# A graph-attention kernel: the residual's bias moves from the DMA queue to the vector engine, the residual tiles move to other buffers, and the instruction planner is revised

## The chip, the cores and the metric

The kernel runs on one core of a Trainium2 chip. The metric is device time in microseconds, from the start of the program to its end; lower is better. The engines are named as in the profile: PE is the tensor engine, DVE the vector engine, ACT the scalar engine, POOL the general-purpose engine, SP the engine that does nothing but issue transfers. [...]

## The reference, cut to what matters

There are 32 graphs of 512 nodes with 512 features. Each graph is normalized, goes through two attention layers, and is added to its input. All arithmetic is in float32.

```python
def gat_layer(x, mask, W, a_src, a_dst, bias, concat):
    xl = (x @ W).reshape(B, N, H, F)
    asrc = einsum('bnhf,hf->bnh', xl, a_src); adst = einsum('bnhf,hf->bnh', xl, a_dst)
    e = leaky_relu(asrc[:, :, None, :] + adst[:, None, :, :], 0.2)
    attn = softmax(where(mask[..., None], e, -1e9), axis=1)
    return einsum('bsdh,bshf->bdhf', attn, xl) (+ bias, heads side by side or averaged)

h = maximum(layernorm(x), 0)
h = elu(gat_layer(h, mask, W1, ..., b1, concat=True))     # 4 heads of 256 features
h = gat_layer(h, mask, W2, ..., b2, concat=False)         # 1 head of 512 features
out = x + h                                               # so out = (attn2 @ xl2) + x + b2
```

## The kernel before, in words

**The work of a graph.** Everything is held in tiles of 128 rows (partitions). A graph goes through four products: `project1` (features by W1, for four heads), `gather1` (attention weights `p` by projected features, per pair of heads), `project2` and `gather2` (the same for the second layer). Nearly all of them are done with seven block products in place of eight, so DVE prepares sums of blocks ahead of a product and PE's partial results are combined as they leave the accumulator banks. In `gather1` the function `sums1` writes two sums of the weights of each head into the buffers `t` (four of them, two heads at a time). In the second layer `sums2` writes sums of `p` into `hs` and differences of the projected features into the buffers `x`.

**The softmax weights.** `Soft.first` computes row scores (buffers `l`, tile `low`) on ACT and DVE, `Soft.second` forms `p`. Row vectors are spread over the partitions through DRAM: a small write and a broadcast read (`das<-as` and `as<-das`, `drr<-rr` and `rr<-drr`), on SP. In most places the mask is added to `p` by a transfer that accumulates, from a copy in DRAM (`p<-dm`, issued on POOL); then ACT takes the exponential.

**The residual.** `residual(b)` loads the four 128-row tiles of the input graph into buffers `xr` on SP, then adds `b2` to each by an accumulating transfer on POOL that reads the 2 KB row of `b2` for all 128 partitions. `gather2` adds each partial product from its accumulator bank into the tile, in place (`xr<-mm,xr` in the profile), and SP writes the tile out. The `xr` buffers (four) also serve `elu` as scratch. For graph 30 other buffers are used, and there DVE adds `b2` already. `residual` runs for all graphs; 124 tiles of 128 go through the path with the accumulating transfer.

**The banks.** In `sevens`, product 3 of a block accumulates in the bank of product 5, so its matmuls may start only when DVE has added product 5's result into the residual tile.

**The rounds.** The loop over `i` works on three graphs at a time: `gather1` of graph i+1, `project1` of i+2, `gather2` of i, `project2` of i+1. A round has 28 + 28 block products of two matmuls each, 14 of four and 14 of two, which makes 196 matmuls. Each matmul shows as two records in the trace.

**The order.** Nothing is issued as it is written down. Every step goes into `Program` as a job with an engine, an assumed duration, and what it reads and writes. `Program.order` then plans: PE's jobs stay in program order; the jobs of the other engines are ranked by how late they may start (`backwards`), placed by a forward pass in time (`forwards`), and this is repeated 12 times; the order with the earliest planned end is issued. The assumed durations and latencies are constants in the code:

```python
CROSS, SAME = 0.15, 0.1
DMA_LEAD, DMA_TAIL, DMA_RATE = 1.2, 1.0, 280e3
```

Of the kernel before, what the change touches and what calls it, by code (L numbers as in the profile page):

```python
# [19 lines left out]
P = 128  # L20
# [24 lines left out]
class Program:  # L45
# [5 lines left out]

    CROSS, SAME = 0.15, 0.1
    DMA_LEAD, DMA_TAIL, DMA_RATE = 1.2, 1.0, 280e3

# [21 lines left out]
    def latency(self, a, b):  # L76

        if self.jobs[a][0] != self.jobs[b][0]:
            return self.CROSS
        return 0.0 if self.jobs[a][0] == "PE" else self.SAME  # L80

    def forwards(self, rank):

        jobs, after = self.jobs, self.after
        n = len(jobs)
        left = [len(job[2]) for job in jobs]
        ready_at, start, landed = [0.0] * n, [0.0] * n, 0.0
        free, soon, ready = defaultdict(float), defaultdict(list), defaultdict(list)
        tensor = deque(j for j in range(n) if jobs[j][0] == "PE")
        for j in range(n):  # L90
            if not left[j] and jobs[j][0] != "PE":
                heappush(soon[jobs[j][0]], (0.0, j))
        done = []
        while len(done) < n:
            j, t = self.next_job(rank, free, soon, ready, tensor, left, ready_at)
            start[j] = t
            free[jobs[j][0]] = t + jobs[j][1]
            done.append(j)
            if jobs[j][4] is not None:
                landed = max(landed, t + jobs[j][1] + self.DMA_LEAD) + jobs[j][4] / self.DMA_RATE  # L100
            for s in after[j]:
                if jobs[j][4] is not None:
                    r = landed + self.DMA_TAIL
                else:
                    r = t + jobs[j][1] + self.latency(j, s)
                ready_at[s] = max(ready_at[s], r)
                left[s] -= 1
                if not left[s] and jobs[s][0] != "PE":
                    heappush(soon[jobs[s][0]], (ready_at[s], s))
        return start, done  # L110

    def backwards(self, rank):
# [9 lines left out]
        while True:  # L122
            for j in found:
                if jobs[j][4] is not None:
                    moving = max(moving, ready_at[j]) + jobs[j][4] / self.DMA_RATE
                    ready_at[j] = moving + self.DMA_LEAD
                if jobs[j][0] != "PE":
                    heappush(soon[jobs[j][0]], (ready_at[j], j))
# [13 lines left out]

    def next_job(self, rank, free, soon, ready, tensor, left, ready_at):

        best = None
        for e in ("PE", "ACT", "DVE", "POOL", "SP"):
# [6 lines left out]
            elif soon[e]:  # L153
                t = max(free[e], soon[e][0][0])
            else:
                continue
            if best is None or t < best[0]:
                best = (t, e)
# [10 lines left out]
    def order(self):  # L169
# [8 lines left out]
        for j in reversed(range(n)):  # L178
            later = self.DMA_LEAD + self.DMA_TAIL + (jobs[j][4] or 0.0) / self.DMA_RATE
            need[j] = max(  # L180
# [6 lines left out]
            if jobs[j][0] == "PE":  # L187
                if pe is not None:
                    need[j] = max(need[j], need[pe] + jobs[pe][1])
                pe = j  # L190
        rank, best, self.tried = need, None, []
        for _ in range(self.ROUNDS):
            back = self.backwards(rank)
            late = [-back[j] - jobs[j][1] for j in range(n)]
            start, done = self.forwards(late)
            end = max(start[j] + jobs[j][1] for j in range(n))
            self.tried.append(end)
            if best is None or end < best[0]:
                best = end, start, done, late
            rank = [-start[j] - jobs[j][1] for j in range(n)]  # L200
        _, self.start, done, self.late = best
        return done

    def emit(self):
# [5 lines left out]
def tile_gat(  # L210
# [113 lines left out]
    def accumulate(size, reads, writes, to, at, cost=0.95):  # L324
        prog.add(
            "POOL", cost, reads, writes,
            lambda: nc.gpsimd.dma_start(to, at, accum_op=OP.add), 1.4 * size,  # L327
        )
# [25 lines left out]
    def weights1():  # L354
        for c in range(2):
            for r in range(2):
                for k in range(KQ):
                    row = (r * KQ + k) * P
                    ix = AT[r, c]
                    dma(  # L360
                        256e3, (), [("w1", ix, k)], w1_sb[:, ix, k, :, 2:],
                        w1[row : row + P, :].rearrange("p (j c f) -> p c j f", j=H // 2, c=2)[:, c],
                    )

    def scores1():

        vk, bc = ps_.take()
        for a, v in enumerate((as1, ad1)):
            for j in range(H // 2):
                dma(  # L370
                    256e3, (), [vk + ("v", a, j)], bc[:, 2 * a + j, :],
                    bass.AP(tensor=v.tensor, offset=v.offset + j * 2 * FH, ap=[[0, P], [1, 2 * FH]]),
# [21 lines left out]
    def weights2():  # L394

        for (r, c), ix in AT.items():
            dma(
                512e3, [("ht", 0, 0)], [("w2", ix)], w2_sb[:, ix, :, 1 - c : W2H - c],
                w2[r * HF // 2 : (r + 1) * HF // 2, c * DO // 2 : (c + 1) * DO // 2].rearrange(
                    "(k p) f -> p k f", p=P  # L400
                ),
            )
        dma(4e3, (), ["b1"], b1_sb[:, 0], b1.rearrange("(c p) -> p c", p=P))
        dve(TINY, ["b1"], ["b1"], nc.vector.tensor_scalar_mul, b1_sb[:, 1], b1_sb[:, 0], -1.0)
        dma(256e3, (), ["b2"], b2_sb, rows_of(b2, P))
        for a, v in enumerate((as2, ad2)):
            lk, bc = ls.take()
            dma(256e3, (), [lk], bc, rows_of(v[0], P))
            for (r, c), ix in AT.items():
# [24 lines left out]
    def load(b):  # L434
        XT[b] = []
        for t in range(NT):
            xk, xt = xs.take()
            dma(256e3, (), [xk], xt, x[b, t * P : (t + 1) * P, :])
            XT[b].append((xk, xt))

    def masks(b):

        for t in range(NT):
            ak, a = adjs.take()
            dma(256e3, (), [ak], a, adj[b, t * P : (t + 1) * P, :])
            dve(
# [10 lines left out]
        if b < B - 1:  # L457
            MASK[b] = mk, md = mds.take()
            dma(512e3, every, [mk], md.rearrange("p t n -> p (t n)"), m.rearrange("p t n -> p (t n)"))
        tk, mt = mts.take()  # L460
# [4 lines left out]
            ),  # L465
            300e3,
        )
# [22 lines left out]
    def norm_turn(b, t):  # L490
# [3 lines left out]
        act(  # L494
            0.62, [xk, sk + (t,)], [xk], hn, hn, AF.Relu,
            bias=st[:, t, S : S + 1], scale=st[:, t, S + A : S + A + 1],
# [13 lines left out]
        else:  # L510
# [3 lines left out]
            act(  # L514
                1.14, [xk], [ak], words.rearrange("p (h f) -> p h f", h=2),
                hn.bitcast(U16).rearrange("p (f h) -> p h f", h=2), AF.Copy,
# [6 lines left out]
                ),  # L523
                200e3,
            )
            act(
                1.14, [xk], [("ht", t, 0), ("ht", t, 1)],
                ht[:, :, t * P : (t + 1) * P].bitcast(U16).rearrange("p k (n h) -> p h k n", h=2),
# [14 lines left out]
    class Soft:  # L543
# [7 lines left out]
        def spread(self, v, keys, rows, to, through):  # L551
# [11 lines left out]
            dma(  # L563
                0, [ok], [dk], dr[:k].rearrange("k (b j) -> b k j", j=32),
                bass.AP(
# [4 lines left out]
            dma(  # L570
                256e3 * rows, [dk], [ok], o[:, :rows].rearrange("p r n -> p (r n)"),
                bass.AP(tensor=dr.tensor, offset=dr.offset, ap=[[0, P], [1, rows * N]]),
# [67 lines left out]
        def second(self, h):  # L640
# [19 lines left out]
            if not here:  # L660
                mk, md = MASK[self.b]
                for us in (0, 1), (2, 3):
                    keys = p_keys(pk, us)
                    accumulate(
                        500e3, keys + [mk], keys,
                        *(t[:, us[0] : us[-1] + 1].rearrange("p t n -> p (t n)") for t in (p, md)),
# [67 lines left out]
    def sevens(left, right, rkeys, put, kh, units, width, order):  # L734
# [3 lines left out]
        for u, n in order:  # L738
            m = units[u][0]
            acc, first = {1: "a", 2: "g", 5: "b", 6: "a", 7: "a", 3: "b", 4: "a"}[n], n in (1, 2, 5)  # L740
            if first:
# [4 lines left out]
            pe(  # L746
                akeys + rkeys(n), [bk], kh * width / 597,
                [
# [48 lines left out]
    def project1_first(zt):  # L797

        for j in range(H // 2):
            zk, z = zt[j]  # L800
            for t in range(NT):
                for c in range(2):
# [5 lines left out]
                           for q in (("w1", AT[r, c], k), ("w1s", AT[r, c], k, j))],  # L808
                        [bk], KT * 0.435,
                        [  # L810
# [29 lines left out]

    def elu(g, places, at, cost):

        keys = [("h1", g, r) for r in range(2)]
        ek, e = xrs.take()
        act(cost, [*places, "b1"], [ek], e, at, AF.Exp, bias=b1_sb[:, 0, g : g + 1], scale=-1.0)
        act(0.54, [ek], [ek], e, e, AF.Relu, bias=1.0, scale=-1.0)
# [6 lines left out]
    def gather1_plain(soft, heads):  # L853

        for h in heads:
            pk, p = soft.p.pop(h)
            for f in range(FPH):
                bk, ps = banks.take()
                for s in range(NT):
# [8 lines left out]
                    )  # L868
                elu(h * FPH + f, [bk], ps, 0.6)
                banks.give(bk)  # L870
# [50 lines left out]
    def gather1(soft, j):  # L921
# [4 lines left out]
        for i, n in PAIR:  # L926
# [5 lines left out]
            if first:  # L932
# [4 lines left out]
            pe(  # L937
                akeys + wkeys, [bk], KQ * M / 597,
                [
# [17 lines left out]
            if n in (3, 4):  # L957
                elu(g, [("h1", g, q) for q in range(2)], h1[:, g, :], 0.54)
        for i in range(2):
# [51 lines left out]

    def residual(b, places=(xrs,) * NT):

        XR[b] = []
        for d in range(NT):
# [5 lines left out]
            halves = [xk, xk + (0,), xk + (1,)]  # L1021
            dma(256e3, (), halves, xr, x[b, d * P : (d + 1) * P, :])
            if places[0] is xrs:
                accumulate(256e3, [xk], halves, xr, rows_of(b2, P))
            else:
                dve(0.59, [xk, "b2"], halves, nc.vector.tensor_add, xr, xr, b2_sb)
            XR[b].append((places[d], xk, xr))
# [27 lines left out]
    def gather2(b, soft, blocks, order=LAST):  # L1055
# [4 lines left out]
        def put(n, u, bk, ps):  # L1060
# [7 lines left out]
            if n == 4 or r == 0 and upper[u[0]] == 0:  # L1068
                upper[u[0]] = -1
                dma(256e3, [xk, xk + (0,), xk + (1,)], (), out[b, d * P : (d + 1) * P, :], xt)  # L1070
                place.give(xk)
# [9 lines left out]
    def gather2_plain(b, soft):  # L1081
# [3 lines left out]
        for d in range(NT):  # L1085
# [8 lines left out]
            dve(0.6, [bk, xk], [xk], nc.vector.tensor_add, xr, ps, xr)  # L1094
            dma(256e3, [xk], (), out[b, d * P : (d + 1) * P, :], xr)
            banks.give(bk)
# [166 lines left out]
```

## Time and profile before

| | |
|---|---|
| runs | 2850.74, 2859.48, 2864.90 us, median 2859.48 |
| profiled execution | 2858.04 us, of which 2856.2 us from the first to the last instruction |
| busy | PE 2774.1, DVE 2584.4, ACT 2306.4, POOL 416.7 us |
| mean granted PE clock | 0.992 |
| transfers | 527.23 MB; the queue fed by POOL moves 191.92 MB |
| DRAM read | 344.72 MB |
| residual bias transfers | 124 of 256 KB, median 5.8 us from issue to landing |
| mask transfers | 304 of 512 KB, median 5.1 us |

The page of a profile gives busy times, a strip of 40 slices, the transfer queues, the chain that ended last, and the costliest groups of instructions. The line number of a group is that of a helper (L333 issues all matmuls, L319 all DVE work, L316 all ACT work, L322 plain transfers, L327 accumulating ones), so groups are told apart by their tiles: `out<-in`, with buffer numbers left out. The tile `xl2` of the second layer shows as `xl`. "Idle before" is the time an engine stood still ahead of an instruction, with the engine and tile whose end released it. A matmul's end is modelled, and a few matmul records are missing.

### The profile page before, as it was taken

Reading aid. Unit: us, or ns where it says so; the run is one execution under the profiler, and the core shown is the slowest. Engines: PE = TensorE matmul, PEld = TensorE weight load, DVE = VectorE, ACT = ScalarE, POOL = GpSimd, SP = SyncE. Lnnn points to the kernel's source line nnn. Section 1 sums busy time; section 2 is a strip of 40 time slices with the busy share of each in tenths; the row PEclk is TensorE's granted clock in tenths of the full one; section 3 lists DMA queues with packets and bytes.
Section 4 is the critical chain, followed back from the end, with each engine's and each line's share of the span. In section 5 each row is a group of like instructions: output and inputs, shape, how many; then the busy total and the mean of one; then the engine's idle time right before and its main releaser. Section 6 shows DMA issues by size and latency. Waiting matters only on the chain. (4 is left out here: it accounts for less than half of the span.)

```text
span 2856.2 us, 41534 instructions
## 1 busy us (share of the span) xinstructions
PE 2774.1 (97%) x12456; PEld 2365.5 (83%) x12456; DVE 2584.4 (90%) x6567; ACT 2306.4 (81%) x4861; POOL 416.7 (15%) x466
## 2 busy tenths in 40 slices
PE   7999999999999999999999999999999999999997
PEld 6668888888888888888888888888888888888875
DVE  7979998989999989899898999999998999999995
ACT  6878798888888888887888888888888888888872
POOL 0011111111111111111111111111111111111100
PEclk9999999999999999999999999999999999999999
DMA  6577777687786777776777877778767778777724
GB/s 204 150 174 182 188 203 188 180 193 194 181 210 181 194 185 191 201 191 182 189 188 182 207 176 183 202 190 206 190 179 194 189 187 215 176 192 191 182 68 128
DMA packets 389455, 527.23 MB, mean 185 GB/s; under 512 B 227184, under 2 KB 231280, under 8 KB 389232
## 3 DMA queue, kind: packets, MB, share of 16 engines
q1 hardware_dynamic: 327600, 332.68, 41.7%
q0 software_dynamic: 61632, 191.92, 30.3%
q8 instruction: 99, 1.62, 0.2%
q14 instruction: 124, 1.02, 0.1%
HBM read 344.72 MB, written 50.79 MB: 138 GB/s over the span
## 5 line engine op out<-in xcount | busy, mean ns | idle before, releaser
L333 PE MATMUL mm<-w_sb,hs 128*128 128x257 f32 (+1 forms) x3024 | 693.2, 383 | 19.4 <-ACT xl L316 10.8
L333 PEld LDWEIGHTS mm<-w_sb,hs 128*128 128x128 f32 x3024 | 574.0, 191 | 113.6 <-ACT xl L316 20.0
L327 POOL DMA_DIRECT2D p<-dm x304 | 267.5, 882 | 2032.1 <-DVE p L319 1034.3
L316 ACT ACTIVATE l<-as,z 128x512 f32<-128x512 f32 x640 | 441.8, 723 | 113.6 <-DMA as<-das 101.7
L316 ACT ACTIVATE l<-l,low 128x512 f32<-128x512 f32 x640 | 459.5, 723 | 71.5 <-DVE low L319 69.0
L316 ACT ACTIVATE p<-p,z 128x512 f32<-128x512 f32 x640 | 432.8, 722 | 103.4 <-DMA p<-dm 75.2
L333 PE MATMUL mm<-p,xl 128*128 128x256 f32 (+1 forms) x2016 | 489.5, 391 | 6.4 <-ACT p L316 3.5
L319 DVE SCALAR_TENSOR_TENSOR p<-rr,z 128x512 f32<-128x512 f32 x640 | 457.8, 745 | 37.2 <-DMA rr<-drr 36.8
L333 PE MATMUL mm<-w_sb,ht 128*128 128x258 f32 x2112 | 481.5, 382 | 2.2 <-ACT xl L316 1.2
L333 PE MATMUL mm<-w_sb,h 128*128 128x257 f32 x2056 | 470.0, 380 | 6.2 <-DVE h L319 4.3
L319 DVE CUSTOM_DVE_ANT_1 l<-l,mt 128x512 f32<-128x512 f32 x640 | 427.4, 683 | 46.2 <-ACT l L316 44.8
L333 PEld LDWEIGHTS mm<-w_sb,ht 128*128 128x128 f32 x2112 | 400.5, 190 | 64.1 <-ACT xl L316 4.0
L333 PEld LDWEIGHTS mm<-p,xl 128*128 128x128 f32 x2016 | 382.9, 190 | 82.6 <-issue 19.4
L333 PEld LDWEIGHTS mm<-w_sb,h 128*128 128x128 f32 x2056 | 389.9, 190 | 65.7 <-DVE h L319 5.3
L316 ACT ACTIVATE xl<-mm 128x258 f32<-128x258 f32 (+2 forms) x752 | 281.7, 384 | 49.0 <-PE mm L333 46.5
L319 DVE TENSOR_TENSOR xl<-xl,mm 128x258 f32<-128x258 f32 x558 | 224.8, 417 | 36.6 <-PE mm L333 28.7
L316 ACT ACTIVATE h<-mm 128x256 f32<-128x256 f32 x480 | 175.4, 379 | 84.2 <-PE mm L333 82.0
L316 ACT ACTIVATE xr<-h,b_sb 128x512 f32<-128x512 f32 x240 | 171.5, 723 | 77.3 <-DVE h L319 76.8
L333 PE MATMUL mm<-t,hs 128*128 128x256 f32 x960 | 218.3, 380 | 1.2 <-ACT h L316 0.9
L333 PEld LDWEIGHTS mm<-t,hs 128*128 128x128 f32 x960 | 183.1, 191 | 27.0 <-ACT h L316 1.3
L319 DVE TENSOR_TENSOR xr<-mm,xr 128x256 f32<-128x256 f32 (+1 forms) x424 | 170.9, 417 | 28.4 <-PE mm L333 19.9
L319 DVE SCALAR_TENSOR_TENSOR h<-h,b_sb,xr 128x512 f32<-128x512 f32 x240 | 175.9, 745 | 20.0 <-ACT xr L316 19.2
(105 smaller groups left out, 3427.6 us busy)
## 6 DMA issues: line engine op xcount, KB each, us to landing
p<-dm POOLq DMA_DIRECT2D x304, 512.0 KB, 5.1
rr<-drr SPq DMA_DIRECT2D x160, 512.0 KB
x<-in_x_dram SPq DMA_DIRECT2D x129, 256.0 KB
adj<-in_adj_dram SPq DMA_DIRECT2D x128, 256.0 KB
as<-das SPq DMA_DIRECT2D x64, 512.0 KB
xr<-in_x_dram SPq DMA_DIRECT2D x124, 256.0 KB
xr<-in_L_gnn_b_dram POOLq DMA_DIRECT2D x124, 256.0 KB, 5.8
out_dram<-xr SPq DMA_DIRECT2D x124, 256.0 KB
```

Source lines behind the costliest of these rows:

```text
L316: prog.add("ACT", cost, reads, writes, lambda: nc.scalar.activation(*a, **k))
L319: prog.add("DVE", cost, reads, writes, lambda: f(*a, **k))
L327: lambda: nc.gpsimd.dma_start(to, at, accum_op=OP.add), 1.4 * size,
L333: f(*a, **k)
```

## The change

Three things are changed.

1. `residual` puts its tiles into the `t` buffers, those of the weight sums of the first layer's `gather1`, in place of `xr`. 
2. `b2` is added to them by DVE (128x512, float32) in place of the accumulating transfer. `b2` is then read from its tile in on-chip memory.
3. The planner gets other constants (durations of transfers in microseconds, latency by pair of engines, transfer lead and tail), a limit on how far ahead transfers are issued, and 40 further passes in which the jobs that caused a planned standstill of PE are ranked earlier. The best of all passes is issued.

Products, their order on PE, and the number of ACT and SP instructions are unchanged: PE 6238, ACT 4223, SP 1233 instructions in both builds; DVE goes from 6505 to 6629, POOL from 471 to 347.

```diff
-    CROSS, SAME = 0.15, 0.1
-    DMA_LEAD, DMA_TAIL, DMA_RATE = 1.2, 1.0, 280e3
+    CROSS, SAME = 0.15, 0.07
+    PAIRS = {("PE", "ACT"): 0.21, ("PE", "DVE"): 0.21, ("DVE", "POOL"): 0.58, ("POOL", "DVE"): 0.4}
+    DMA_LEAD, DMA_TAIL, AHEAD = 0.8, 2.0, 3.5
...
-            j, t = self.next_job(rank, free, soon, ready, tensor, left, ready_at)
+            j, t = self.next_job(rank, free, soon, ready, tensor, left, ready_at, landed - self.AHEAD)
...
+    def sooner(self, rank, start, cause):
+        jobs, lost, free = self.jobs, {}, 0.0
+        for j in range(len(jobs)):
+            if jobs[j][0] != "PE":
+                continue
+            gap, free = start[j] - free, start[j] + jobs[j][1]
+            d = cause[j]
+            while gap > 0.05 and d is not None and start[j] - start[d] < self.SPAN:
+                lost[d] = max(lost.get(d, 0.0), gap)
+                d = cause[d]
+        return [r - self.GAIN * lost.get(j, 0.0) for j, r in enumerate(rank)]
+
+    SPAN, GAIN = 60.0, 2.0
...
+            if e in ("SP", "POOL"):
+                t = max(t, hold)
...
+        _, start, _, cause, rank = best
+        for _ in range(self.REPAIRS):
+            rank = self.sooner(rank, start, cause)
+            start, cause = look(rank)
...
+    REPAIRS = 40
...
-    def residual(b, places=(xrs,) * NT):
+    def residual(b, places=(ts_,) * NT):
...
-            dma(256e3, (), halves, xr, x[b, d * P : (d + 1) * P, :])
-            if places[0] is xrs:
-                accumulate(256e3, [xk], halves, xr, rows_of(b2, P))
-            else:
-                dve(0.59, [xk, "b2"], halves, nc.vector.tensor_add, xr, xr, b2_sb)
+            dma(0.75, (), halves, xr, x[b, d * P : (d + 1) * P, :])
+            dve(0.59, [xk, "b2"], halves, nc.vector.tensor_add, xr, xr, b2_sb)
```

Of the jobs' assumed durations, some are changed too: a plain 256 KB transfer from 0.91 to 0.75 us, the mask transfer of 512 KB from 2.5 to 2.2 us, the transposing ones from 0.71 to 1.27 and from 1.07 to 2.5 us, and four ACT jobs.

## The prediction

> **What bounds the kernel now.** I read the busy times first, then PE by slices, then who ended PE's waits in the steady stretch, then single waits in the order of time.
>
> ```profile
> PE 2774.1 (97%) x12456; PEld 2365.5 (83%) x12456; DVE 2584.4 (90%) x6567; ACT 2306.4 (81%) x4861; POOL 416.7 (15%) x466
> ```
>
> PE is the bound and DVE is next. PE's 82 us of idle time are not spread evenly, as three of the 40 slices show (columns: PE, PEld, DVE, ACT, POOL busy with records, clock, transfers):
>
> ```profile
> 428.40:499.80 71.40, 67.53 (x303) 57.93 (x302) 63.17 (x160) 57.15 (x119) 11.83 (x13) 0.98 0.73 188
> 1642.30:1713.70 71.40, 67.96 (x303) 57.82 (x302) 64.56 (x167) 57.14 (x132) 10.88 (x12) 0.98 0.70 176
> 2356.40:2427.80 71.40, 71.40 (x331) 62.37 (x330) 66.31 (x167) 59.91 (x125) 13.51 (x15) 1.00 0.84 215
> ```
>
> A slice without a wait holds 331 records, 0.2157 us each. The first slice shows 3.9 us idle but lacks 28 records, 6.0 us: a wait costs more than it shows, since the matmuls after it are slower. The steady stretch is 214.2 to 2713.4 us, rounds 1 to 29; PE idles 36.7 us there. One matmul comes once a round, the first of `mm<-xl,hs` in `gather2`: from 373.83 to 2641.05 us it passes 26 rounds, **87.2 us each**. 392 records at 0.2157 us are 84.6 us, so a round loses 2.6 us and 29 rounds lose 75 us, twice the idle time shown. From 1948.02 to 2033.05 a round took 85.03 us, so the chip can do one with hardly a wait. PE's waits in this stretch (us in total, times, longest):
>
> ```profile
> PE mm L333 <- DVE hs L319: 13.1, 5, 3.6
> PE mm L333 <- DVE xr L319: 11.8, 17, 2.3
> PE mm L333 <- ACT xl L316: 5.7, 12, 0.9
> PE mm L333 <- ACT h L316: 5.0, 6, 1.8
> PE mm L333 <- ACT p L316: 0.2, 1, 0.2
> ```
>
> The second row is followed back in one round (timeline of POOL, DVE, PE):
>
> ```profile
> 1155.39 0.86 POOL L327 DMA_DIRECT2D xr<-in_L_gnn_b_dram  x1 [7.13 <-DMA xr<-in_x_dram]
> 1159.62 0.42 DVE L319 TENSOR_TENSOR xr<-mm,xr 128x256 f32<-128x256 f32 x1 [2.00 <-DMA xr<-in_L_gnn_b_dram]
> 1160.10 1.13 PE L333 MATMUL mm<-xl,hs 128*128 128x256 f32 x4 [2.34 <-DVE xr L319]
> ```
>
> POOL waits for x, the bias transfer lands some 4 us later, DVE's addition waits for it, and product 3 waits for DVE to clear product 5's bank. In the built order 10.3 us of DVE work (mostly 9.5 to 11.5) stand between the `elu` that frees `xr` and the first addition into it. A load (issued by 1147.22, awaited by POOL until 1155.39, so up to 8.2 us) and a bias transfer (5.8 us median) don't fit. The first row, at 458.38, 1330.22, 1683.56 and 2204.52 us (10.8 us), comes from the same place: POOL's queue then holds the layer-2 mask transfers between bias transfers, `p` lands late, ACT's exponential and DVE's sums into `hs` follow late.
>
> [...]0.98 where 3.4 to 3.9 us are idle, 1.00 elsewhere. [...]the trace has 684 to 685 ns for graph 30's bias additions, but neighbours start 0.60 us apart (2816.60, 2817.20, 2817.80), and that is the price. [...]mask and bias share POOL's queue; its 191.92 MB are 304 x 512 KB + 124 x 256 KB.
>
> **The change part by part.** PE's order is the same, instruction by instruction, so all differences are in when its operands come.
>
> *Removed:* 124 bias transfers. POOL loses 124 x 0.90 = 111 us of issuing, which covers nothing (POOL is 15% busy). Its queue loses 32.5 of 191.9 MB. The chain above ends with the load. I let `DVE xr` fall from 11.8 to 1 us, and `DVE hs` from 13.1 to 4 (bounds 1 and 10: the mask transfers still take 5.1 us).
>
> *Added:* 124 DVE additions x 0.61 = 76 us; 116 serve rounds 0 to 28, 71 us, or 2.44 a round. DVE idles 190.1 us in the steady stretch, 6.6 a round, and the additions lie in that. In the order nearly all stand 7 to 15 us of DVE work ahead of their first use, so they are not on the path of PE unless DVE is full or x is late. If x is late, the addition holds up everything behind it on DVE, sums for PE among it. From the release of `t` by PE (product 6 of `gather1`) to the addition, PE and DVE work in the order leaves 8.7 to 13 us, in one round 5.1 to 6.2; against 8.2 us for a load at worst this exposes 0 to 3 us in one round. Graph 0's four fall where DVE waits 0.8 to 2.0 us for each matmul group at 34 to 42 us; their four loads go before the adjacency loads of the head, bounded at +3 us, taken as 0.
>
> *Moved to `t`:* on SP the four loads now wait for PE, and `as<-das` and the mask copy stand behind them in most rounds. ACT's waits for `as<-das` (88.9 us in the stretch) may grow; ACT has 420 us idle there, so 0. The next `sums1` must wait until the tile is written out: 5.4 us of DVE work or more stand between. A write is not timed by the page; the last one ends the span 2.7 us after its issue, so 0, upper bound 1 us a round.
>
> *The planner:* its effect shows only in the order. For each matmul of rounds 1 to 29 that waits for DVE, I summed the DVE work from DVE's own last waits for PE up to the awaited instruction, and took off the PE work between. Before, the DVE work is larger in 44 of 1049 places, after in 7 of 1128, the additions included. For ACT it is 0 and 2. So waits set by DVE's queue are mended; waits set by transfers are not in this count. I let PE's waits on ACT fall from 10.9 to 8, and add 4 for new ones.
>
> Sum for the rounds: 36.7 - (1 + 4 + 8 + 4) = 19.7 us less idle; each counts twice (75/36.7 = 2.0), **39 us**.
>
> *The end:* before the last product PE waits 7.98 us for the weights of graph 31. SP held that chain up:
>
> ```profile
> 2805.93 0.52 SPq L322 DMA_DIRECT2D das<-as  x1
> 2809.32 3.79 SPq L322 DMA_DIRECT2D out_dram<-xr  x3
> 2813.20 0.38 SPq L322 DMA_DIRECT2D as<-das  x1
> ```
>
> In the new order `as<-das` directly follows `das<-as`: it saves 4 to 5 us. Against that, around `gather1` of graph 31 (2749 to 2763 us) the count above grows from 6.9 to 8.7 us. Net 2 us saved, bounds 5 saved and 2 lost. The head is taken as 0, bounds 4 either way.
>
> Sum: 2858.0 - 39 - 2 = 2817 against the profiled execution's own time; the median of the runs is 1.4 us above that: **2818 us**. About 0.5% is what a measurement of this kernel can tell from no change: 14 us, so 2845 and 2874 are the borders.
>
> **The rivals.**
>
> *The bound passes to DVE (slower).* Of DVE's 190 us idle in the rounds only 36.0 are waits for PE (`xl` 21.0, `xr` 4.7, `h` 3.8, `p` 3.3, `hs` 3.2); the others are latency, as 40.4 for ACT's `l` and 31.0 for `rr<-drr`. If these stay, 71 us of additions fill only the 36, and 35 come on top, with PE's waits kept in another place: 2858 + 35 = 2893. It decides as soon as DVE's idle time, less the additions, cannot sink below 6.6 - 2.4 = 4.2 us in a round of 87.2. For it: DVE would be over 95% busy. Against it: the additions have 10 us of leeway and can stand in latency waits, and the order's count fell.
>
> *The waits change their releaser (no difference).* Mask transfers, not bias transfers, set `hs`; the additions wait for x where DVE waited for the bias. Then `xr` alone falls, by about half: 6 us x 2, less nothing at the end, 2847; with 1 or 2 us more at the head, 2849. For it: the `p<-dm` row of 5.1 us stays. Against it: in all of the long waits bias transfers stood beside the masks.
>
> *The planner's passes do nothing.* Then the order would be as late as before: the 44 to 7 speaks against it, and its time is that of the case before this.
>
> **How the numbers follow.** Forecast 0.72, no difference 0.16, DVE bound 0.12. The forecast's own range is 2791 (all 29 rounds at 85.03, so 29 x 2.17 = 63, and 5 at the end) to 2840 (hs and ACT mended by half, 2 lost at the end). The range of 8 in 10 reaches on over the case of no difference: 2791 to 2858; it leaves out the DVE case and a little below. Faster by over 0.5%: 0.73, within 0.16, slower 0.11.
>
> **What would show it.** Right: no row of bias transfers on POOL, its queue at about 159 MB; `DVE xr` (now `DVE t` on `xl,hs`) near 1 us; DVE busy about 2660 us; rounds of 85.9 us; the last wait of PE near 3 to 4 us. Wrong: DVE waiting for `t<-in_x_dram` by more than 20 us in total; `DVE hs` still above 10; rounds above 87.

## The result and the profile after

The change makes the kernel faster: **2807.54 us** as the median of four runs (2807.30 to 2816.68), against 2856.45 us for four runs of the kernel before on the same chip; the ratio is **0.9834, 95% interval 0.9801 to 0.9867**. The forecast was 2818 us with a range of 2791 to 2858. The profiled execution took 2807.30 us against 2858.04 us, 50.7 us less; the sum of the prediction had said 41.

I read the page of the kernel after first: engines, the queue that POOL feeds, and the mask transfers (the last column is the median from issue to landing, in us).

```profile
PE 2758.2 (98%) x12456; PEld 2364.6 (84%) x12456; DVE 2640.6 (94%) x6691; ACT 2307.5 (82%) x4861; POOL 311.7 (11%) x342
...
q0 software_dynamic: 43776, 159.40, 24.0%
...
p<-dm POOLq DMA_DIRECT2D x304, 512.0 KB, 5.3
```

PE stays the bound. POOL's queue carries only the mask transfers, and they land no sooner than before (5.3 against 5.1 us), with a sixth of the queue's bytes taken away. DVE is busy 56 us longer.

Next PE's waits in the steady stretch of the kernel after, 214 to 2665 us (us in total, times, longest):

```profile
PE mm L368 <- DVE hs L354: 3.4, 3, 1.9
PE mm L368 <- DVE h L354: 1.3, 2, 1.0
PE mm L368 <- ACT h L351: 0.7, 2, 0.4
PE mm L368 <- DVE xl L354: 0.6, 2, 0.3
PE mm L368 <- ACT xl L351: 0.5, 2, 0.3
PE mm L368 <- DVE t L354: 0.4, 2, 0.3
PE mm L368 <- ACT p L351: 0.2, 1, 0.2
```

That is 7.1 us where 35.8 us were. All sources of before have shrunk, and DVE's `h` and `xl` are new with 1.9 us together: the bank's wait for the residual (`xr`, now `t`) from 11.8 to 0.4, `hs` from 13.1 to 3.4, those on ACT from 10.9 to 1.4 us.

**Where the 50.7 us lie.** The first matmul of `mm<-x,hs` in each round marks the rounds in PE's timeline. Before, 28 rounds pass from 197.35 to 2636.24 us, 87.1 us each; after, from 191.49 to 2587.36 us, 85.57 us each. So the rounds save 2438.89 - 2395.87 = 43.0 us, the head 197.35 - 191.49 = 5.9 us, and what follows the last mark up to the end of the span 1.9 us (219.96 less 218.04). After the change 17 of the 28 rounds take 85.0 or 85.1 us; before, 3 did.

**DVE, with four more additions in a round.** One stretch of nearly eleven rounds in the kernel after (busy times of PE, PEld, DVE, ACT, POOL with records, then clock, transfer share, GB/s):

```profile
981.90:1893.60 911.70, 911.70 (x4203) 797.17 (x4202) 882.34 (x2216) 778.07 (x1641) 111.10 (x121) 1.00 0.70 184
```

PE has no idle time and DVE is 96.8% busy: of 85 us it idles 2.7. Its own waits tell what the additions displaced. First two rows of the kernel before (214 to 2713 us), then four of the kernel after (200 to 2620 us):

```profile
DVE l L319 <- ACT l L316: 40.4, 65, 1.9
DVE p L319 <- DMA rr<-drr: 31.0, 33, 2.6
```

```profile
DVE xl L354 <- PE mm L368: 19.7, 43, 1.0
DVE l L354 <- ACT l L351: 8.8, 19, 1.5
...
DVE t L354 <- DMA t<-in_x_dram: 5.8, 7, 2.0
...
DVE p L354 <- DMA rr<-drr: 4.8, 7, 1.8
```

The waits for ACT's `l` and for the broadcast `rr` were latency: while one operand was under way DVE stood still. They lost 58 us together. The additions have taken their place, and x is late for them by 5.8 us in all. DVE's waits for PE on `xl`, which the rival of a DVE bound wanted to see filled first, are hardly touched (21.0 and 19.7).

### The profile page after: what moved, and what is told of

The parts are those of the page before. It is cut to its first block, busy times and chain, and to the rows that moved or that the text cites. A ratio compares the mean times of both kernels' runs of the same rounds, so it can differ in the third digit from the quotient of the medians.

```text
span 2805.4 us, 41284 instructions
## 1 busy us (share of the span) xinstructions
PE 2758.2 (98%) x12456; PEld 2364.6 (84%) x12456; DVE 2640.6 (94%) x6691; ACT 2307.5 (82%) x4861; POOL 311.7 (11%) x342
## 4 chain that ended last, share of the span: by engine, by line
PE 85%; DVE 7%; ACT 3%; DMA 3%; issue 1%; SPq 0%; POOL 0%; DVEq 0%; ACTq 0%; POOLq 0%
PE mm L368 85%; DVE p L354 2%; ACT l L351 1%; DMA x<-adj 1%; DVE h L354 1%; DMA rr<-drr 1%; DVE l L354 1%; DMA p<-dm 1%; DVE hs L354 1%; DVE t L354 1%; ACT p L351 1%; DVE xl L354 0%; ACT adj L351 0%; ACT xl L351 0%; ACT xr L351 0%
## 5 line engine op out<-in xcount | busy, mean ns | idle before, releaser
L368 PE MATMUL mm<-w_sb,hs 128*128 128x257 f32 (+1 forms) x3024 | 690.9, 383 | 11.8 <-ACT xl L351 7.1
L354 DVE TENSOR_TENSOR t<-mm,t 128x256 f32<-128x256 f32 (+1 forms) x424 | 171.5, 416 | 15.6 <-PE mm L368 14.9
L368 PE MATMUL mm<-xl,p 128*128 128x256 f32 (+1 forms) x752 | 181.6, 391 | 4.2 <-ACT p L351 4.0
```

Source lines behind the costliest of these rows:

```text
L354: prog.add("DVE", cost, reads, writes, lambda: f(*a, **k))
L368: f(*a, **k)
```

## The experiments

All twelve runs, each with its ratio to the kernel before on the same chip (e8_end_only ran once and has none). On the other chips the kernel before had medians of 2862.34 to 2866.68 us, so ratios are compared, not medians. The mean round is that between the marks in its profile. The last column is the count of the prediction, made from the built order: places in rounds 1 to 29 where the DVE work ahead of an awaited instruction exceeds PE's work beside it (a dash: not given). The expectations give microseconds on the scale of the first chip, so they are best read by ratio, times 2856.45 us: e3_same_order_no_bias then lies at the lower edge of its rival's range, and only e13_pool_add falls clearly outside all of its ranges.

| run | what differs | median us | ratio (95%) | round us | places |
|---|---|---|---|---|---|
| before | | 2856.45 | 1 | 87.1 | 44 |
| after | | 2807.54 | 0.9834 (0.9801, 0.9867) | 85.57 | 7 |
| e3_same_order_no_bias | before, bias transfers not issued | 2851.04 | 0.9958 (0.9943, 0.9972) | 86.98 | 44 |
| e12_no_addition | after, additions not issued | 2811.81 | 0.9809 (0.9787, 0.9832) | 85.45 | 7 |
| e1_planner_only | new planner, old residual | 2869.81 | 1.0025 (1.0010, 1.0039) | 87.66 | 91 |
| e2_residual_only | old planner, new residual | 2854.25 | 0.9963 (0.9949, 0.9977) | 86.56 | 41 |
| e4_dve_bias_in_xr | after, residual in `xr` | 2835.03 | 0.9907 (0.9880, 0.9934) | 86.99 | – |
| e5_pool_bias_in_t | after, bias by transfer | 2846.43 | 0.9941 (0.9924, 0.9958) | 86.57 | 30 |
| e6_no_repairs | after, no further passes | 2823.02 | 0.9864 (0.9826, 0.9901) | 85.75 | 29 |
| e7_repairs_only | after, old constants | 2823.62 | 0.9860 (0.9807, 0.9913) | 86.23 | 5 |
| e11_gain1 | after, other passes | 2806.74 | 0.9792 (0.9768, 0.9816) | 85.51 | 3 |
| e9_two_ops | after, a second DVE operation | 2866.24 | 1.0010 (0.9992, 1.0029) | 87.15 | – |
| e13_pool_add | after, POOL adds | 2940.66 | 1.0258 (1.0234, 1.0282) | 89.85 | 45 |
| e8_end_only | before, one step moved at the end | 2865.59 | one run | 87.41 | 44 |

### Are the bias transfers what PE waited for? (e3_same_order_no_bias)

```diff
-                accumulate(256e3, [xk], halves, xr, rows_of(b2, P))
+                prog.add("POOL", 0.95, [xk], halves, lambda: None, 1.4 * 256e3)
```

> The kernel before, every engine in its old order, but the 124 bias transfers are planned and not issued; b2 is left out of the output. No addition takes their place on DVE. It is the price of the transfers alone. Theory: PE's waits for xr additions (11.8 us) and for hs in gather2 (10.8 us) go almost wholly, some 20 us idle, counted twice: 2815 to 2825 us. Rival, the order of DVE's own work sets those waits: 2845 to 2857 us, with the once-a-round wait of mm<-xl,hs still there.

The order of all other instructions stays that of the kernel before. Measured: 2851.04 us, 0.42% less (0.28 to 0.57%), about 12 us, not 39. PE's waits in 214 to 2660 us, and three of the long ones in PE's timeline (start, duration, ..., idle before and its releaser):

```profile
PE mm L333 <- DVE hs L319: 12.0, 5, 3.0
PE mm L333 <- ACT xl L316: 10.8, 13, 2.6
PE mm L333 <- DVE xr L319: 7.6, 12, 1.3
```

```profile
460.66 3.72 PE L333 MATMUL mm<-x,hs 128*128 128x256 f32 x16 [2.53 <-DVE hs L319]
...
1686.92 3.72 PE L333 MATMUL mm<-x,hs 128*128 128x256 f32 x16 [2.96 <-DVE hs L319]
...
2204.45 5.12 PE L333 MATMUL mm<-x,hs 128*128 128x256 f32 x16 [2.72 <-DVE hs L319]
```

In the kernel before these three matmuls waited 3.63, 3.00 and 2.72 us, at 458.38, 1683.56 and 2204.52 us. So with no bias transfer anywhere the same places still wait for `hs`, the first of them 1.1 us less. The row of `xr` falls from 11.8 to 7.6 us. DVE's own waits tell what is left of it: before, DVE waited 7.8 us for bias transfers, in nine places, and here it waits for no transfer of the residual, for x neither. So the 7.6 us come from the other work and waits that stand ahead in DVE's order. The size of the fall is not sharp, since one execution differs from the next: e8_end_only, with the bias transfers and the same order in these rounds, shows 16.4 us for this row. In the profiled execution here (2856.07 us, one of the slower of its 20) the wait for ACT's `xl` is 10.8 us (5.7 before, 8.2 in e8_end_only), and PE's waits come to 35.7 us, as in the kernel before. Most of the waits belong to the order; the transfers stood beside them and added a part. The waits at the head (6.12 us at 51.96, 4.25 at 115.57, 4.10 at 186.97) are those of the kernel before too.

### Do the additions cost anything? (e12_no_addition)

```diff
-            dve(0.59, [xk, "b2"], halves, nc.vector.tensor_add, xr, xr, b2_sb)
+            prog.add("DVE", 0.59, [xk, "b2"], halves, lambda: None)
```

> The whole change in its order, the 124 bias additions planned and not issued; b2 is left out of the output. If they lie in DVE's waits, as the prediction has it: 2800 to 2810 us, no more than 8 us below the whole change. If they show as the second operation did (59 us for 76): the rounds that are not yet 85.0 us become so, 2785 to 2797 us; more is not to be had, since 28 rounds are on average 0.6 us above that.

The order is that of the kernel after. The four additions of graph 30 go out with the others, so 128 are left out, not 124. Measured: 0.9809 against 0.9834, with overlapping intervals: no cost of the additions that these runs can tell. DVE idle time comes back instead (window row, then DVE's first two waits in 200 to 2620 us):

```profile
981.90:1893.60 911.70, 911.16 (x4195) 794.11 (x4195) 858.88 (x2170) 775.25 (x1636) 111.86 (x121) 1.00 0.70 184
```

```profile
DVE xl L354 <- PE mm L368: 41.7, 68, 2.6
DVE l L354 <- ACT l L351: 36.1, 56, 2.1
```

Without the additions DVE works 23.5 us less in this stretch and waits that much longer, for PE's `xl` and ACT's `l`. PE's 911.70 and 911.16 us are the same.

### Residual or planner? (e1_planner_only, e2_residual_only)

```diff
-    def residual(b, places=(ts_,) * NT):
+    def residual(b, places=(xrs,) * NT):
...
-            dve(0.59, [xk, "b2"], halves, nc.vector.tensor_add, xr, xr, b2_sb)
+            if places[0] is xrs:
+                accumulate(1.15, [xk], halves, xr, rows_of(b2, P))
+            else:
+                dve(0.59, [xk, "b2"], halves, nc.vector.tensor_add, xr, xr, b2_sb)
```

> The new planner with the residual as before: tiles in xr, bias by the accumulating transfer. If the bias transfers are the late chain, as the prediction's sum has it, the wait of product 3 for DVE's addition stays and the time is 2845 to 2865 us. If the planner's order carries the gain, the time is 2810 to 2825 us. In the order itself DVE's work is larger than PE's between in 91 places of rounds 1 to 29 (before 44, after the whole change 7), which speaks for the slow end: 2860 us.

```diff
-    def residual(b, places=(xrs,) * NT):
+    def residual(b, places=(ts_,) * NT):
...
-                accumulate(256e3, [xk], halves, xr, rows_of(b2, P))
+            dve(0.59, [xk, "b2"], halves, nc.vector.tensor_add, xr, xr, b2_sb)
```

> The new residual (t buffers, bias by DVE) with the planner and its constants as before. If taking the bias transfers away carries the gain: 2815 to 2830 us, with PE's waits for the residual's additions under 2 us in total and its waits for hs at 2 to 5 us. If the planner carries it: 2845 to 2860 us, since DVE's work is larger in 41 places of the order, nearly as many as before. If DVE's added 76 us come through: 2880 us or more.

The first diff is against the kernel after, the second against the kernel before. Measured: 2869.81 us (ratio 1.0025) for the new planner with the old residual, 2854.25 us (0.9963) for the new residual with the old planner. Their gains are together 0.1%, where the whole change gains 1.7%: **neither part is worth much without the other**. PE's waits with the new planner and the old residual (214 to 2660 us):

```profile
PE mm L368 <- DVE xr L354: 23.7, 25, 3.5
PE mm L368 <- DVE hs L354: 21.1, 10, 5.0
```

Both are worse than in the kernel before, and DVE waits 13.7 us for the bias transfer (7.8 before, 12.5 in e8_end_only). I read it so, without a run that tests it apart: the old residual's chain (buffer free, load, transfer, addition into the tile) does not fit, and this order of the other work did not mend it. That the planner's new limit on early transfers holds the old chain up stays possible. With the new residual and the old planner PE has no wait for the residual's additions at all; it waits 12.7 us for `hs`, in 19 short waits, 8.8 for ACT's `xl` and 6.2 for `p`.

### Buffers or bias? (e4_dve_bias_in_xr, e5_pool_bias_in_t)

```diff
-    def residual(b, places=(ts_,) * NT):
+    def residual(b, places=(xrs,) * NT):
```

> The whole change, but the tiles stay in the xr buffers shared with elu. If the buffers matter little: 2805 to 2815 us, as the whole change. If the earlier release of t is what gives the loads time: 2825 to 2845 us, with DVE waiting for the x loads by more than 15 us in total, since an xr buffer comes free only some 10 us of DVE work ahead of gather2.

```diff
-            dve(0.59, [xk, "b2"], halves, nc.vector.tensor_add, xr, xr, b2_sb)
+            if places[0] is ts_:
+                accumulate(1.15, [xk], halves, xr, rows_of(b2, P))
+            else:
+                dve(0.59, [xk, "b2"], halves, nc.vector.tensor_add, xr, xr, b2_sb)
```

> The new planner, the tiles in the t buffers, the bias still by the accumulating transfer. Theory O, that the room which the order leaves DVE sets the time: 30 places of rounds 1 to 29 leave DVE too little, so like the residual alone, 2835 to 2855 us. Theory B, that the early release of t is the gain: 2805 to 2820 us, the 76 us of DVE additions being saved as well.

With the kernel after and e1_planner_only these fill a square, all under the new planner:

| ratio to before | bias by transfer | bias by DVE |
|---|---|---|
| residual in `xr` | 1.0025 | 0.9907 |
| residual in `t` | 0.9941 | 0.9834 |

No two intervals meet across a row or a column. The other buffers give 0.84% or 0.73%, the bias on DVE 1.18% or 1.07%: within the intervals the two effects add. So the buffers are a full part of the gain, which the prediction did not price by itself. But each of the four kernels is planned anew, so each effect contains the order that the planner found for it. In `xr` with the bias on DVE, DVE waits for the load of x only 1.9 us (3 times), and not the 15 us that one theory wanted; the place of the cost is in PE's waits on ACT, 24.6 us for `p` and `xl` in a profiled execution that was the slowest of its eight runs (2846.27 us).

### Constants or passes? (e6_no_repairs, e7_repairs_only, e11_gain1)

```diff
-    REPAIRS = 40
+    REPAIRS = 0
```

> The whole change without the 40 further passes: new residual, new constants and the limit on transfers. Theory O: 29 places, so 2835 to 2850 us. Theory C, that constants closer to the measured durations carry the planner's part: 2805 to 2820 us.

```diff
-    CROSS, SAME = 0.15, 0.07
-    PAIRS = {("PE", "ACT"): 0.21, ("PE", "DVE"): 0.21, ("DVE", "POOL"): 0.58, ("POOL", "DVE"): 0.4}
-    DMA_LEAD, DMA_TAIL, AHEAD = 0.8, 2.0, 3.5
+    CROSS, SAME = 0.15, 0.1
+    PAIRS = {}
+    DMA_LEAD, DMA_TAIL, AHEAD = 1.2, 1.0, 1e9
+    DMA_RATE = 280e3
```

The assumed durations of e7_repairs_only are those of before as well.

> New residual and the 40 further passes, with the constants, latencies and durations of the kernel before and no limit on transfers. Theory O: 5 places leave DVE too little (7 in the whole change), so 2805 to 2820 us. Theory C: the passes mend standstills of a plan that is not the chip's, so 2835 to 2855 us.

```diff
-    SPAN, GAIN = 60.0, 2.0
+    SPAN, GAIN = 60.0, 1.0
...
-    REPAIRS = 40
+    REPAIRS = 200
```

> The whole change with another setting of the passes: 200 in place of 40, each raising ranks by half as much. It gives another order, with 3 places that leave DVE too little (7 in the whole change). If the count is what matters and the change's result is no accident of one order: 2795 to 2815 us, ratio 0.980 to 0.985. If the whole change hit a lucky order among many: 2820 to 2840 us.

With the new residual, either half of the planner gives 0.986, from 0.9963 without either; both give 0.9834. Read by ratio, Theory C fits e6_no_repairs alone and Theory O fits e7_repairs_only alone. The last step lies within the intervals. Other passes, and so another order, give 2806.74 us, ratio 0.9792 with an interval that meets that of the kernel after: the gain does not hang on one lucky order, and a better one than the kernel after is not shown.

The count of places follows the time only roughly. 5 places took 86.23 us a round and 29 took 85.75: the count knows DVE's queue alone, and the order with old constants leaves PE waiting 10.4 us for ACT's `xl`, 19 times.

### How far is DVE from being the bound? (e9_two_ops)

```diff
-            dve(0.59, [xk, "b2"], halves, nc.vector.tensor_add, xr, xr, b2_sb)
+            dve(0.59, [xk, "b2"], halves, both, xr, b2_sb)
...
+    def both(xr, b):
+        nc.vector.tensor_add(xr, xr, b)
+        nc.vector.tensor_max(xr, xr, xr)
```

> The whole change in its order, with each bias addition followed by a maximum of the tile with itself, which changes nothing in the output: 124 more DVE instructions of 0.61 us, 2.4 us a round. In the perfect rounds of the whole change DVE idles 2.7 us of 85. If DVE has become the bound there: 2840 to 2890 us, rounds of 86.5 us or more, most of the 76 us showing. If the additions lie in waits and PE stays the bound: at most 2820 us.

The second operation leaves the values as they are; the order is unchanged. It follows the additions of graph 30 too, so there are 128 of it. Measured: ratio 1.0010 against 0.9834, so this second helping of 128 operations costs 1.76%, about 50 us, and takes the whole gain. The stretch of the window row above, and the first of PE's waits (214 to 2660 us):

```profile
981.90:1893.60 911.70, 901.77 (x4136) 781.97 (x4137) 892.23 (x2229) 764.26 (x1609) 108.11 (x117) 1.00 0.69 180
```

```profile
PE mm L368 <- DVE xl L354: 27.9, 24, 2.4
```

DVE idled 4.9 us in 85 without additions, 2.7 with them; a second 2.44 us do not fit, and it now idles 1.8 in 85 while PE waits for it. The mechanism of the slower rival is real and begins within one more operation per tile, at least in an order that was not planned for it; an order made with the second operation was not tried.

### Could POOL add? (e13_pool_add)

```diff
-            dve(0.59, [xk, "b2"], halves, nc.vector.tensor_add, xr, xr, b2_sb)
+            prog.add(
+                "POOL", 1.2, [xk, "b2"], halves,
+                lambda xr=xr: nc.gpsimd.tensor_tensor(xr, xr, b2_sb, op=OP.add),
+            )
```

> The whole change with the bias addition on POOL instead of DVE (same operands, planned at 1.2 us, an order of its own). DVE is spared 76 us. If DVE's load is what still limits the rounds: 2790 to 2805 us. If the room in the order limits (45 places here, 7 in the whole change), or the mask transfers wait behind the additions on POOL: 2825 to 2850 us.

Measured: 2940.66 us, ratio 1.0258, the slowest of all and outside both forecasts. POOL's addition takes 1.53 us where 1.2 were planned, and DVE is busy for longer: 2707.3 us, against 2573.1 where nobody adds (e12_no_addition). How much of the loss is the order, planned with the short duration, was not tested apart. One place in the timeline (DVE and POOL):

```profile
1086.76 3.74 DVE L354 SCALAR_TENSOR_TENSOR h<-h,b_sb,xr 128x512 f32<-128x512 f32 x1
...
1087.13 2.80 POOL L1060 TENSOR_TENSOR t<-t,b_sb 128x512 f32<-128x512 f32 x2
...
1090.41 0.68 DVE L354 CUSTOM_DVE_ANT_1 l<-l,mt 128x512 f32<-128x512 f32 x1
```

A DVE instruction with a mean of 0.743 us in the kernel after lasts 3.74 us, to 1090.50, shortly after POOL's second addition ends at 1089.93. It is single instructions that are long: of the 240 of this kind the median is 746 ns in both kernels, the longest 4901 ns here and 756 ns in the kernel after. The 360 of `h<-h,mm`, which read an accumulator bank, stay at 427 ns or less (422 in the kernel after). What holds the long ones up the runs do not show; DVE's record starts 0.37 us ahead of POOL's, and spans on POOL are rough.

### The step at the end alone (e8_end_only)

```diff
+        for j in self.first:
+            done.remove(j)
+            done.insert(1 + max(done.index(d) for d in jobs[j][2]), j)
...
+            if self.b == B - 1 and self.layer == 2 and through is das:
+                prog.first.append(len(prog.jobs) - 1)
```

> The kernel before with one step moved: for the last graph the broadcast read as<-das stands directly behind das<-as on SP, ahead of the three writes of the output. The prediction took 4 to 5 us for it: PE's last wait, 7.98 us before, should be 3 to 4 us, and from the last project2 to the end 4 to 5 us less. If the chain is held up elsewhere, the wait stays at 7 us or more. The whole time moves by less than a single run can tell.

One run: 2865.59 us, where the kernel before had a median of 2866.68 us on that chip. SP now issues `as<-das` at 2817.14, 2.8 us after `das<-as` in place of 7.3. From the timelines of SP, ACT and PE:

```profile
2817.14 0.33 SPq L326 DMA_DIRECT2D as<-das  x1
...
2827.56 0.72 ACT L320 ACTIVATE l<-l,low 128x512 f32<-128x512 f32 x1 [4.96 <-DVE low L323]
...
2843.35 16.57 PE L337 MATMUL mm<-xl,p 128*128 128x512 f32 x32 [7.03 <-ACT p L320]
```

PE's last wait falls by 1 us only, from 7.98 to 7.03. The issue is 4.5 us sooner, but ACT then waits 4.96 us for DVE, whose reduction of `l` starts at 2826.83, behind sums of other tiles in its order.

## Why the prediction was right, and which of its steps were not

**Held.** PE stays the bound; the additions lie in DVE's latency waits (e12_no_addition); the queue at 159 MB; DVE waits 5.8 us for x, under the 20 set as the mark; rounds of 85.57 us for 85.9; DVE busy 2640.6 us for about 2660. The prediction was nearer to right in its total than in its reasons.

**Failed: the step "Removed".** It put the fall of `DVE xr` from 11.8 to 1 and of `DVE hs` from 13.1 to 4 down to the missing bias transfers, because these stood beside the waits in the timeline. Both fell as forecast or further (0.4 and 3.4), but taking the transfers alone away left 7.6 and 12.0. What the runs show in its place is a joint effect of the new residual (its buffers and its shorter chain, 0.8% and 1.1%) and of a new order planned with it: with the new residual and the old planner the wait for `xr` is gone, while `hs` stays at 12.7 and the gain is 0.37%. The rival "the waits change their releaser" described the removed transfers correctly (its 2847 to 2849 us are 0.3 to 0.4% below the 2858 it starts from; e3_same_order_no_bias gained 0.42%). As a forecast for the whole change it was wrong, since the order moved too. The prediction had the evidence, 44 places falling to 7, and gave it no term of its own. The third rival took the planner's passes alone for the planner: without them e6_no_repairs still reaches 0.9864, with the new constants.

**Mis-sized: the sum for the rounds.** The forecast was 36.7 - 17 = 19.7 us less idle, times 2.0. Measured: from 36.7 to 7.5 us (2455.0 us less PE's 2447.5 in 209 to 2664 us), 29.2 us less, and 43.0 us saved, so 1.5 each. Of the 4 us for new waits 1.9 came, and ACT's waits fell to 1.4 and not 8. The factor was too high in part because it took 84.6 us as a round without waits; 17 rounds in which hardly a wait is left took 85.0, which makes it 1.7 (29 times 2.2 us over 36.7 us). The two errors of the term offset each other, which is luck: 39 was said, 43.0 measured.

A factor on idle time also has the wrong shape. Two windows of 3 us in the kernel before (the third number from the end is the granted clock), behind a wait of 3.63 us at 458.38 and one of 1.42 us at 1330.22:

```profile
458.00:461.00 3.00, 2.62 (x6) 2.18 (x7) 2.97 (x6) 2.33 (x7) 0.35 (x1) 0.52 0.79 132
...
1332.00:1335.00 3.00, 2.86 (x14) 1.96 (x12) 3.00 (x11) 1.17 (x4) 0.00 (x0) 1.00 0.78 233
```

In such windows the clock also falls, to between 0.52 and 0.71, behind waits of 3.00 us (at 1683.56; 0.52 in 1684 to 1687), 2.72 us (at 2204.52; 0.62 in 2205 to 2208) and 2.34 us (at 1160.10; 0.71 in 1160 to 1163), and to 0.64 in 499 to 502 behind the one of 1.94 us at 499.51 in the kernel after; behind 2.29 us (at 1469.46; 1469 to 1472) and 1.80 us (at 2506.89; 2507 to 2510) it stays at 1.00. Sixteen matmuls of `mm<-x,hs` take 5.25 to 5.41 us behind the three longest waits, where they take 3.61 to 3.72 us without one: by estimate 1.7 us on top of each long wait. So the prediction read the slices wrongly when it put 0.98 down to 3.4 to 3.9 us of idle time and 1.00 to all else. The one from 1142 to 1214 us has 2.8 us idle and 0.98, the one from 2499 to 2570 us has 3.5 us idle, in shorter waits, and 1.00. The lower clock goes with some of the long single waits here, and not with the idle time of a slice. A length of wait at which it falls can't be read from these runs: it is 0.64 behind 1.94 us and 1.00 behind 2.29 us, and in e3_same_order_no_bias the sixteen matmuls of `mm<-x,hs` take 3.72 us behind a wait of 2.96 us and 5.12 us behind one of 2.72 us. The steady stretch has four waits with a lower clock behind them before and one after, by estimate some 5 of the 13.8 us saved beyond the idle time; where the others lie is open.

**Missed: the head.** It was taken as 0 with bounds of 4 us; the two profiled executions differ by 5.9. The wait of 6.11 us for `hs` at 51.11 is now 2.68 at 48.74, and those of 4.26 us at 114.39 and 3.77 at 185.25 are gone, while 4.40 and 2.77 us are new at 56.43 and 67.95. As e3_same_order_no_bias kept the old waits, this does not come from the transfers. It does not repeat well either: e12_no_addition, with the order and the buffers of the kernel after, reaches the first mark at 196.04 us, 1.3 us ahead of the kernel before, and e6_no_repairs, with these buffers in another order, at 198.58. How much of the 5.9 us belongs to the order is open.

**The end: right in its net, wrong in a part.** Net 2 us were forecast and 1.9 measured. In the kernel after, SP issues the pair as forecast and PE's last wait is 3.85 us, inside the 3 to 4 named:

```profile
2761.33 0.52 SPq L357 DMA_DIRECT2D das<-as  x1
2762.96 0.33 SPq L357 DMA_DIRECT2D as<-das  x1
```

```profile
2785.66 16.04 PE L368 MATMUL mm<-xl,p 128*128 128x512 f32 x32 [3.85 <-ACT p L351]
```

But "it saves 4 to 5 us" was said of SP's step, and that step alone saved 1: DVE was next in line, in its order of before. I take it that the rest needed DVE's work to move as well; no run moves it alone. The loss set against it came: around `gather1` of graph 31 PE waits 5.9 us (2.32, 1.42, 0.41, 0.86, 0.56, 0.35), 2.4 more than before.

**The slower rival.** It set the point at 4.2 us of DVE idle in a round, as if latency waits could not be filled. DVE went to 2.7 us with PE at full load, so the point was wrong for this change. With 1.8 us left in e9_two_ops PE waits for DVE, so there it lies below 2.7.

## What to carry to other kernels

A transfer seen beside a wait is not its cause until the wait goes with it: leave the transfer out at the same order and look whether the wait stays. An order and the shape of the work in it belong together: here the shorter chain gained 0.37% with the old planner, the new planner lost 0.25% with the old chain, and both gained 1.7%. Idle time of a busy engine that is latency took independent work here at no cost that shows (0.9834 with 128 additions of 0.6 us, 0.9809 without, in overlapping intervals), up to a point somewhere between 128 and 256 operations (with 256 the ratio is 1.0010), in one order.

## What the runs showed of the hardware that was not expected

POOL's additions cost DVE more than the same additions on DVE: 128 of them lengthen DVE's busy time by 134 us (2707.3 less 2573.1), where doing them on DVE adds 67.5 us (2640.6 less 2573.1). The mean of `h<-h,b_sb,xr` goes from 743 ns in the kernel after to 897 ns in e13_pool_add:

```profile
L354 DVE SCALAR_TENSOR_TENSOR h<-h,b_sb,xr 128x512 f32<-128x512 f32 x240 | 212.1, 897 | 9.7 <-ACT xr L351 9.5
```

And removing 32.5 MB of accumulating transfers from a queue did not move the landing of the other transfers in it in one direction. Their median is 5.1 us in the kernel before and 6.1 in e5_pool_bias_in_t, with these transfers; without them it is 5.2 in e2_residual_only, 5.7 in e4_dve_bias_in_xr and 5.3 in the kernel after. The orders differ in these.
